# Layer 1 of a four-layer graph attention kernel: the products among the first eleven tiles are formed in the last group of layer 0's gathers, and layer 1 is cut into five blocks

## The chip, the cores and the metric

The kernel runs on one core of one Trainium2 chip. The metric is the device time of one execution in microseconds (us). Times of several runs are given as a median with the lowest and the highest.

## The reference

Four graph attention layers over 3327 nodes with 256 features, one shared adjacency matrix, each followed by a residual addition and a layer norm:

```python
# x: (3327, 256) fp32; adj: (3327, 3327) int32, symmetric, about 1% ones and the diagonal
x = _layernorm(x + _L0_gnn_ref(x, adj, ...))   # GATv2: a . leaky_relu(src_i + tgt_j), softmax over j
x = _layernorm(x + _L1_gnn_ref(x, adj, W, a))  # GAT, one head
x = _layernorm(x + _L2_gnn_ref(x, adj, ...))   # GAT, one head, no leaky_relu
x = _layernorm(x + _L3_gnn_ref(...))           # two GAT layers of four heads of 64

def _L1_gnn_ref(h, adj, W, a):
    Wh = h @ W.T
    s1, s2 = Wh @ a[:256], Wh @ a[256:]
    e = leaky_relu(s1[:, None] + s2[None, :], 0.2)
    e = where(adj == 0, -1e9, e)
    return softmax(e, axis=1) @ Wh
```

In layer 1 row i of the result is a weighted mean of the projected rows j that are neighbours of i. The kernel uses exp(leaky_relu(s1 + s2)), which up to a factor of i is exp(s2) times the larger of a number of i (the "rate") and a number of j. So one vector instruction, max with a scalar of j and then times the adjacency, gives a tile of weights, and a product with the rows of j gives sums over j.

## The kernel before

The nodes are cut into 26 tiles of 128 rows. The program has two parts.

**Layer 0** (`sparse0`) uses that a node has few neighbours. The tiles are handled in four groups, `SETS = (4, 7, 9, 6)`. For a group, `neighbours(s)` finds each row's neighbours by scanning the adjacency, and orders the rows by number of neighbours. Then for each tile POOL gathers, neighbour by neighbour, one row of a table in memory for each of the 128 rows (`gather`, line 912: one indirect transfer of 128 rows of 260 numbers). Gathers are put into parts of up to four; there are 237 parts, of which the last group has 55. One loop goes over the parts. At step q it issues the gathers of part q + 8 (`LEAD`), computes the scores of part q on VectorE (lines 932 and 938), and does what is due at that step. After a tile's last part come the softmax weights (line 976) and `combine`: ScalarE scales gathered rows (line 1014) and TensorE adds them up by products with the identity (line 1017). `put_back` writes a tile's result to memory by an indirect transfer of POOL (line 1051), and `take` reads a group's rows of h back. What is due at a step is listed by `at_step(q, what)`, and within the stage all five engines keep the order in which the program emits instructions.

A tile with the longest lists has an excess: neighbours beyond the seats of a row are spread over other rows (`excess`, `gather_excess`, `score_excess`). `gather_excess` issues two indirect transfers (line 836): the neighbours' rows, and the "own" rows of 773 numbers. Own rows, of the tiles too (`gather_own`, line 897), have four buffers.

While the last group is gathered, the rows of the first 20 tiles (the first three groups, `EARLY`) are already projected for layer 1: `turn_next` transposes a tile on TensorE, `project_next` multiplies it with the weights and sends the features to memory (`feats_d`, line 1154) and the rates of a finished block (`rate1_d`). The first 11 tiles are taken from step `begins[3]` on, one per two steps, and the nine of the third group from `begins[3] + 38` on.

**Layers 1 to 3** (`layers`) are dense. Layers 1 and 2 (`one_head`) go over four blocks of 7, 7, 6 and 6 target tiles. For each source tile j the adjacency of the block comes to the chip (in layer 1 as int32, `ask`, line 135, and ScalarE makes a bf16 copy, line 1651, which it stores to `at_d` for the later layers); VectorE forms the weights (line 1624), and TensorE adds one product of 128x128 by 128x257 to each target tile's sum (line 1718). The adjacency tiles and the weight tiles share eight buffers (tag `e`), the bf16 copies have three. Layer 1's first block reads the features of the first 20 tiles from `feats_d`, three tiles ahead; those of the last six tiles are made within that block, by a list of pieces of work (`pending`) of which one or two are done per source tile (`work_off`). Each later block in the same way carries the norm and the projection for layer 2 of the block before. At the end of a block come the evictions (lines 1739 and 1740). Then, after the first block, the layer 2 object is made: its weights are loaded and VectorE forms two columns of them (`dots`, lines 164 and 165). Layer 3 (`many_heads`) has four heads, twice.

The order of TensorE is that of the program throughout. The other engines keep the program's order until the end of layer 1's first block (`in_order.close()`, `sp_order.close()`); after it a scheduler orders them.

The lines that carry layer 1's loop:

```python
for j in range(nt):
    at = adjacent(j, b, layer is l1)
    e = layer.weigh(j, b, at, 0)
    for s, it in enumerate(block):
        nc.tensor.matmul(accs[s][:pn, : dim + 1], e[:pj, s * P : s * P + pn], f[:pj, : dim + 1], ...)
```

## Time and profile before

| | |
|---|---|
| time, median of 3 runs | 2938.57 us (2932.43 to 2940.5) |
| the profiled execution's own time | 3369.56 us |
| its span, first to last instruction | 3367.8 us |
| TensorE matmul (PE) busy | 2374.6 us, 71% |
| VectorE (DVE) busy | 2134.7 us, 63% |
| ScalarE (ACT) busy | 855.2 us, 25% |
| GpSimd (POOL) busy | 993.0 us, 29% |
| first and last row gather start | 83.6 and 1727.7 us |
| layer 1's products | 1782.9 to 2121.4 us |

The shares are means over stages that have different limits. In a row of the order in time the numbers are start and duration in us, then engine, line and operation, and in brackets how long the engine was idle before it and what ended the wait; "issue" is a wait for which the profile shows nothing, "remote" one whose releaser it cannot name. PEld is TensorE's weight load, which overlaps its matmuls. PEclk is the granted TensorE clock as a share of the full one. An fp32 product is two MATMUL instructions. The profiled execution and the runs that are timed are different executions.

### The profile page before, as it was taken

The page shows a single profiled execution, that of the slowest core. Times are in us where ns is not written, and L with a number is a line of the kernel's source. Part 1 is how long each engine was busy: PE and PEld are TensorE (multiplying, and loading weights), DVE is VectorE, ACT ScalarE, POOL GpSimd, SP SyncE. Part 2 cuts the span into 40 slices and gives each one's busy share as a digit, 9 for nine tenths or more (in the row PEclk, how much of TensorE's full clock was granted, in tenths as well). Part 3 has the DMA queues.
Part 4 walks back from the last instruction along what each step waited for, and adds up shares of the span by engine and source line. Part 5 has one row for each costly group of instructions (what it writes and reads, how often), then busy time and mean ns, then how long its engine had stood idle before and what let it go on. Part 6 is the DMA issues. An engine that isn't in the chain of part 4 may idle for free.

```text
span 3367.8 us, 47149 instructions
## 1 busy us (share of the span) xinstructions
PE 2374.6 (71%) x16703; PEld 1584.2 (47%) x16732; DVE 2134.7 (63%) x5589; ACT 855.2 (25%) x2381; POOL 993.0 (29%) x1061
## 2 busy tenths in 40 slices
PE   7156365453345433444458999999999999999997
PEld 4024243342233332333347788888545656744442
DVE  6278457565466664443554555210689999989997
ACT  3034233232224231322344344111011011111211
POOL 2734644655545666645730000000000000000000
PEclk8557667676666766666779999999999999999998
DMA  7464444433434333324326767333222222222211
GB/s 226 135 178 142 131 121 123 138 103 90 111 101 126 106 91 99 95 78 138 102 62 189 245 197 201 91 107 103 82 64 62 77 75 77 61 67 58 57 48 47
DMA packets 183863, 370.64 MB, mean 110 GB/s; under 512 B 35772, under 2 KB 124707, under 8 KB 182596
## 3 DMA queue, kind: packets, MB, share of 16 engines
q1 hardware_dynamic: 103994, 178.49, 18.9%
q0 software_dynamic: 51008, 155.70, 16.6%
q10 hardware_dynamic: 28618, 33.33, 2.9%
q8 instruction: 137, 2.24, 0.3%
q14 instruction: 106, 0.87, 0.1%
HBM read 327.52 MB, written 46.23 MB: 111 GB/s over the span
## 4 chain that ended last, share of the span: by engine, by line
PE 47%; DVE 16%; issue 13%; another core or an unknown queue 11%; POOL 6%; DMA 4%; ACT 3%; ACTq 0%; DVEq 0%; SPq 0%; POOLq 0%
PE acc L1768 16%; PE acc L1718 13%; PE acc L1776 8%; PE acc L1017 5%; POOL g L912 5%; DVE y L938 4%; DVE y L932 3%; PE misc L1552 2%; DVE e L1624 2%; DVE cand L579 2%; ACT g L1014 1%; DVE found L587 1%; DVE cand L589 1%; DMA at_d<-at 1%
## 5 line engine op out<-in xcount | busy, mean ns | idle before, releaser
L912 POOL DMA_INDIRECT g<-table_d,lst x894 | 851.6, 953 | 417.8 <-issue 259.3
L1624 DVE SCALAR_TENSOR_TENSOR e<-rate,feat,at 128x896 f32<-128x896 f32 (+4 forms) x832 | 843.4, 1078 | 59.7 <-PE acc L1776 47.8
L1768 PE MATMUL acc<-e,feat 128*32 128x384 f32 (+2 forms) x6656 | 692.1, 514 | 2.5 <-DVE e L1624 1.1
L1017 PE MATMUL acc<-g,ident 128*128 128x256 f32 x1766 | 542.0, 468 | 211.6 <-ACT g L1014 86.1
L1017 PEld LDWEIGHTS acc<-g,ident 128*128 128x128 f32 x1766 | 418.2, 242 | 321.3 <-issue 101.3
L938 DVE SCALAR_TENSOR_TENSOR y<-y,a_ps 128x257 f32<-128x257 f32 x894 | 324.6, 418 | 280.6 <-remote 228.0
L1768 PEld LDWEIGHTS acc<-e,feat 128*32 128x32 f32 x6656 | 306.4, 110 | 295.7 <-issue 157.5
L1776 PE MATMUL acc<-e,feat 128*32 128x384 f32 (+3 forms) x3328 | 383.9, 512 | 0.0
L1014 ACT ACTIVATE g<-g,w 128x256 f32<-128x256 f32 x883 | 366.9, 495 | 13.4 <-issue 8.0
L553 PE MATMUL v<-code,leads 65*128 65x512 bf16 (+1 forms) x182 | 88.7, 487 | 326.4 <-remote 134.3
L1718 PE MATMUL acc<-feat,e 128*128 128x257 f32 (+2 forms) x1352 | 303.7, 382 | 8.8 <-DVE inv L1739 5.6
L932 DVE TENSOR_TENSOR y<-g,minus_ps 128x1028 f32<-128x1028 f32 (+2 forms) x233 | 273.0, 1172 | 24.8 <-issue 20.3
L1718 PEld LDWEIGHTS acc<-feat,e 128*128 128x128 f32 (+2 forms) x1352 | 255.1, 191 | 46.3 <-issue 8.0
L1718 PE MATMUL acc<-feat,at 128*128 128x257 bf16 (+2 forms) x2028 | 239.2, 275 | 9.0 <-DMA at<-at_d 8.8
L579 DVE MAX8 cand<-v 128x8 f32<-128x104 f32 (+2 forms) x858 | 168.2, 261 | 98.4 <-issue 90.8
L1776 PEld LDWEIGHTS acc<-e,feat 128*32 128x32 f32 (+1 forms) x3328 | 161.9, 110 | 131.4 <-issue 88.9
L1718 PEld LDWEIGHTS <-at 128*128 128x128 bf16 (+2 forms) x2028 | 199.4, 100 | 43.3 <-DMA at<-at_d 9.5
L1624 DVE SCALAR_TENSOR_TENSOR e<-rate,feat,at_i 128x896 f32<-128x896 f32 (+2 forms) x104 | 112.1, 1079 | 93.8 <-DMA at_i<-in_adj_t_dram 50.8
L1017 PE MATMUL acc<-own_of,ident 128*128 128x256 f32 x52 | 28.6, 651 | 197.9 <-ACT own_of L1014 63.1
L553 PEld LDWEIGHTS <-leads 65*128 65x128 bf16 x182 | 22.8, 125 | 264.2 <-remote 134.2
L1604 POOL DMA_DIRECT2D rate3b_d<-rate_rows x4 | 2.1, 520 | 450.9 <-ACT rate_rows L1603 450.9
L251 POOL TENSOR_TENSOR rstds<-rstds,minus_half 128x7 f32<-128x7 f32 (+1 forms) x8 | 12.1, 1507 | 385.4 <-DVE rstds L250 385.4
(252 smaller groups left out, 1909.1 us busy)
## 6 DMA issues: line engine op xcount, KB each, us to landing
adj_i<-in_adj_dram SPq DMA_DIRECT2D x75, 512.0 KB
at<-at_d SPq DMA_DIRECT2D x150, 224.0 KB
at_i<-in_adj_t_dram SPq DMA_DIRECT2D x50, 448.0 KB
at<-at_d SPq DMA_DIRECT2D x75, 192.0 KB
at<-at_d SPq DMA_DIRECT2D x75, 191.8 KB
g<-table_d,lst POOLq DMA_INDIRECT x894
at_d<-at ACTq DMA_DIRECT2D x50, 224.0 KB
at_i<-in_adj_t_dram SPq DMA_DIRECT2D x25, 384.0 KB
```

The lines of the kernel that those rows point to most:

```text
L553: nc.tensor.matmul(v[:, :w], leads[:, b, :], code[:, :w], start=True, stop=False)
L579: nc.vector.max(spread[:, c0 + c, :], view(v[:, :w]))
L912: nc.gpsimd.indirect_dma_start(out=g[:, k - k0, :], out_offset=None, in_=table_d[:, :], in_offset=bass.IndirectOffsetOnAxis(ap=entry["lst" ...
L932: nc.vector.tensor_tensor(y, rows, minus_src[:, None, :].to_broadcast([P, m, dim + 1]), op=ALU.max)
L938: nc.vector.scalar_tensor_tensor(y, y, 1.0, a_ps[:, : dim + 1], op0=ALU.mult, op1=ALU.mult, accum_out=sc)
L1014: nc.scalar.activation(rows, rows, AF.Copy, scale=w[:, k : k + 1])
L1017: nc.tensor.matmul(dst, ident, rows, start=start, stop=stop)
L1552: nc.tensor.matmul(pacc[:pn, : dim + self.extra], ht[:, k, :pn], self.weight[:, k, :], start=(k == 0), stop=(k == kc - 1),)
L1624: nc.vector.scalar_tensor_tensor(e[:pn, : c1 - c0], self.rate[b][:pn, h_of, : c1 - c0], q, at[:pn, : c1 - c0], op0=ALU.max, op1=ALU.mult,)
L1718: nc.tensor.matmul(accs[s][:pn, : dim + 1], a[:pj, s * P : s * P + pn], f[:pj, : dim + 1], start=(j == 0 and part == 0), stop=(j == nt - 1 ...
L1768: nc.tensor.matmul(accs[x][p][q : q + 32, : hi - lo], f[:pj, at0 : at0 + 32], es[at0 // hd][:pj, lo:hi], start=(j == 0), stop=(j == nt - 1),)
L1776: nc.tensor.matmul(accs[x][pairs][h_of * 32 : (h_of + 1) * 32, : hi - lo], f[:pj, dim + h_of : dim + h_of + 1].to_broadcast([pj, 32]), es[ ...
```

## The change

Layer 1 is cut into five blocks instead of four, along the groups: tiles 0-4, 5-10, 11-14, 15-19 and 20-25 (`blocks1`). They are handled in the order 11-14, 0-4, 5-10, 15-19, 20-25 (`order1`).

The products whose source and target tiles are both among the first eleven (`KNOWN` = 11) are formed in the last group of layer 0. The targets are taken in sets of up to three (0-2, 3-4, 5-7, 8-10), for each set the eleven source tiles one per step, 44 steps from `begins[3] + 2` on. `ask_early` loads adjacency and features two steps ahead on SP's queue, `weigh_early` makes the bf16 copy on ScalarE, stores it to `at_d` and forms the weights on VectorE, `add_early` makes up to three products one step later, and `keep_early` copies finished sums out and stores them to `part_d`. In layer 1 the blocks 0-4 and 5-10 then start at source tile 11; their parts are loaded at the block's start and added by products with the identity at source tile 15.

The first eleven tiles are projected 25 steps earlier, with the loads that this takes.

The own rows of the excess are no longer gathered: `send_own` makes them by a product with a permutation from the tile's own rows.

The layer 2 object is made at source tile 9 of layer 1's first block and the layer 3a object at source tile 15; their `dots` become single steps (`fold`) at one per source tile from four tiles later. At the end of a layer 1 block the first two edge tiles of the next block are formed ahead of the evictions (`ready`), and the sums of successive blocks take PSUM banks in rotation. Rates of layer 1's five blocks share four buffers: block 20-25 uses that of block 11-14.

The core of the diff:

```diff
+    KNOWN = sum(SETS[:-2])
+    blocks1 = []
+    for lo, hi in ((0, KNOWN), (KNOWN, EARLY), (EARLY, nt)):
+        count = -(-(hi - lo) // 6)
+        ends = [lo + (hi - lo) * c // count for c in range(count + 1)]
+        blocks1 += [list(range(a, b)) for a, b in zip(ends, ends[1:])]
+    order1 = sorted(range(len(blocks1)), key=lambda b: (blocks1[b][0] != KNOWN, b))
...
-                for dst, src, x in ((own, own_d[s], 1), (g[:, 0, :], table_d, 0)):
-                    nc.gpsimd.indirect_dma_start(
-                        out=dst, out_offset=None, in_=src[:, :],
-                        in_offset=bass.IndirectOffsetOnAxis(ap=over["rows"][:, x : x + 1], axis=0),
-                    )
+                nc.gpsimd.indirect_dma_start(
+                    out=g[:, 0, :], out_offset=None, in_=table_d[:, :],
+                    in_offset=bass.IndirectOffsetOnAxis(ap=over["rows"][:, :1], axis=0),
+                )
+
+            def send_own(s):
+                over = extras[s]
+                over["own"] = early_bank()
+                nc.tensor.matmul(
+                    over["own"][:, : dim + 1], over["forth"], held[s, 0]["own"][:, : dim + 1],
+                    start=True, stop=True,
+                )
...
+            def ask_early(m):
...
+                t = find.tile([P, PIECE], I32, tag="adj_i", name="at_f", bufs=3)
+                f = t[:, BANK : BANK + dim + 2].bitcast(F32)
+                copy_rows(nc.sync, t[:, :w], adj_t[j * P : (j + 1) * P, lo : lo + w])
+                nc.sync.dma_start(f, feats_d[j * P : (j + 1) * P, :])
+                asked1[m] = t, f
+
+            def weigh_early(m):
...
+                at = find.tile([P, 3 * P], BF16, tag="cand", name="at1")
+                nc.scalar.copy(at[:, :w], t[:, :w])
+                nc.scalar.dma_start(at_d[j * P : (j + 1) * P, lo : lo + w], at[:, :w])
+                x = m % 3 * 3 * P
+                e = formed1[m] = state1["e"][:, x : x + w]
+                nc.vector.scalar_tensor_tensor(
+                    e, state1["rate"][:, :w], f[:, dim + 1 : dim + 2], t[:, :w],
+                    op0=ALU.max, op1=ALU.mult,
+                )
+
+            def add_early(m):
...
+                if j == 0:
+                    state1["accs"] = [early_bank() for _ in trio]
+                for s, acc in enumerate(state1["accs"]):
+                    nc.tensor.matmul(
+                        acc[:, : dim + 1], e[:, s * P : (s + 1) * P], f[:, : dim + 1],
+                        start=(j == 0), stop=(j == KNOWN - 1),
+                    )
+
+            def keep_early(m):
+                for s, it in enumerate(pairs1[m][0]):
+                    y = find.tile([P, dim + 1], F32, tag="minus", name="part1")
+                    nc.scalar.copy(y, state1["accs"][s][:, : dim + 1])
+                    nc.scalar.dma_start(part_d[it * P : (it + 1) * P, :], y)
...
-            at = begins[len(SETS) - 1]
+            at = begins[len(SETS) - 1] - 2 * KNOWN - 3
...
+            at = begins[len(SETS) - 1] + 2
+            at_step(at - 2, ask_early, 0)
+            at_step(at - 1, ask_early, 1)
+            for m, (trio, j) in enumerate(pairs1):
+                at_step(at, add_early, m - 1)
+                if j == 0 and m:
+                    at_step(at + 1, keep_early, m - 1)
+                    at += 1
+                at_step(at, weigh_early, m)
+                at_step(at, ask_early, m + 2)
+                at += 1
...
-                rate = (rates if b else head_p).tile(
-                    [P, heads, len(blocks[b]) * P], F32, tag=f"r{b}", name="rate"
+                blocks = self.blocks
+                x = self.order.index(b) % 4
+                rate = (rates if x else head_p).tile(
+                    [P, self.nh, len(blocks[b]) * P], F32, tag=f"r{x}", name="rate"
                 )
...
-            for b, block in enumerate(blocks):
+            for turn_b, b in enumerate(layer.order):
+                block, first = layer.blocks[b], turn_b == 0
+                skip = first_of(layer, b)
                 work_until(lambda: not layer.leaky or layer.rate[b] is not None)
-                accs = [bank(s) for s in range(len(block))]
-                for j in range(nt):
+                accs = [bank((used + s) % 7) for s in range(len(block))]
+                used += len(block)
+                parts = ask_parts(block) if skip else ()
+                for j in range(skip, nt):
...
+                    if skip and j == skip + LATER:
+                        for acc, y in zip(accs, parts):
+                            nc.tensor.matmul(
+                                acc[:, : dim + 1], ident, y, start=False, stop=False
+                            )
...
-                    elif j >= LATER:
+                    elif j >= skip + LATER:
                         work_off()
+                    if first and j in make:
+                        made.append(make[j]())
+                        folds += [(j + 4 + i, step) for i, step in enumerate(made[-1].fold())]
+                    while folds and folds[0][0] <= j:
+                        folds.pop(0)[1]()
                 work_until(lambda: not pending)
-                in_order.close()
+                if layer is l1 and turn_b + 1 < len(layer.order):
+                    then = layer.order[turn_b + 1]
+                    work_until(lambda: layer.rate[then] is not None)
+                    at0 = first_of(layer, then)
+                    for j in range(at0, at0 + 2):
+                        ready[j] = fetched(j, then)
...
-        one_head(l1, second, (7,))
-        l2 = made[0]
-        l3a = Layer("l3a", "f", heads, True, load_heads(l3_w1, l3_a1), rate_d=rate3_d[0])
-        one_head(l2, lambda: l3a, (7,))
+        one_head(l1, {9: second, 15: third}, (7,))
+        l2, l3a = made
+        one_head(l2, {}, (7,))
```

## The prediction

> **What bounds the kernel now.** I read the page first (span, the rows by slice), then the busy time by stretch, then POOL's rows, then the chain of waits and the order of instructions around layer 1.
>
> ```profile
> span 3367.8 us, 47149 instructions
> PE   7156365453345433444458999999999999999997
> POOL 2734644655545666645730000000000000000000
> PEclk8557667676666766666779999999999999999998
> ```
>
> Two kernels in one: for 21 slices no engine is full and TensorE is granted 0.6 to 0.7 of its clock; from there PE is full to the end. The busy time by stretch (us, and instructions in brackets, for PE, PEld, DVE, ACT, POOL; then clock, DMA share, GB/s) puts the border at 1782 us:
>
> ```profile
> 1374.00:1728.00 354.00, 148.19 (x513) 115.94 (x512) 166.67 (x593) 95.04 (x278) 211.17 (x222) 0.67 0.39 104
> 1728.00:1782.00 54.00, 43.69 (x194) 34.04 (x192) 32.43 (x109) 36.09 (x115) 2.66 (x3) 0.99 0.11 31
> 1782.00:1877.00 95.00, 87.61 (x402) 74.21 (x402) 37.65 (x61) 31.98 (x59) 4.63 (x6) 1.00 0.77 241
> 1877.00:1960.00 83.00, 77.37 (x355) 66.83 (x356) 49.69 (x96) 33.76 (x58) 1.50 (x1) 0.96 0.72 215
> ```
>
> The first row is the last group's gathers, the second their tail, the third layer 1's first block. In the gather stage POOL issues one indirect transfer after another; two rows of its order in time, and the statistics of the line:
>
> ```profile
> 1510.59 0.95 POOL L912 DMA_INDIRECT g<-table_d,lst  x1 [0.30 <-issue]
> 1511.84 0.94 POOL L912 DMA_INDIRECT g<-table_d,lst  x1 [0.30 <-issue]
> ...
> L912 POOL DMA_INDIRECT g<-table_d,lst x894: 941/949/1562, 83.6 to 1727.7; - x179
> ```
>
> One costs 0.95 + 0.30 = 1.25 us. There are 894 + 8 + 26 + 26 + 22 = 976, so POOL's floor is 1220 us; the profiled stage (83.6 to 1728) took 1644. The profiled execution took 3369.56 us (span 3367.8 and 1.8 around it), 431 more than the median of 2938.57. Layers 1 to 3 (1782.9 to 3367.8, 1585 us) run with PE full, so I place the 431 us ahead of them: without profile 2938.6 - 1.8 - 1585 - 83.6 - 54 (tail) leaves 1214 us for the gathers, POOL's floor within 6 us. The stage without profile is then POOL's alone, and the long stalls that the waits put down to nobody belong to the profile:
>
> ```profile
> DVE y L938 <- remote: 228.0, 43, 27.2
> POOL g L912 <- PE acc L1017: 64.9, 21, 18.8
> ```
>
> This inference carries the forecast; a rival below drops it.
>
> **Layer 1 before.** The order of PE in time:
>
> ```profile
> 1849.09 27.57 PE L1718 MATMUL acc<-feat,e 128*128 128x257 f32 x126
> 1882.26 2.05 PE L1718 MATMUL acc<-feat,e 128*128 128x257 f32 x4 [5.59 <-DVE inv L1739]
> ...
> 2026.24 2.77 PE L1718 MATMUL acc<-feat,e 128*128 128x257 f32 x12
> 2028.84 1.03 PE L1552 MATMUL misc<-l2w,turned 128*128 128x257 f32 x4
> ```
>
> A product is two instructions; six take 2028.84 - 2026.24 = 2.60 us, 0.434 each. Layer 1 runs from 1782.9 to 2121.4, 338.5 us, with 26 x 26 = 676 products (293.4). The first block ends at 1876.7: 182 products are 79.0 of its 93.8, so 14.8 for projecting the last six tiles; 5.6 idle; then 494 products are 214.4 of 239.1, so 24.7 for layer 2's projections.
>
> **The change, part by part.**
> *Products moved.* 11 x 11 = 121 leave layer 1: -52.5. Eleven additions of a 128x257 part, same shape as a product: +4.8.
> *The block boundary.* Layer 2's and 3a's weight columns (dots) are now formed inside the first block, so the 5.6 us go: DVE then had waited for l_att and done both layers' dots ahead of the evictions. The next block's first two edge tiles are now formed before the evictions; the other boundaries cost 0.4 to 0.6 each and I leave them. Sum so far: -53.3.
> *The first block gets shorter than what feeds it.* It has 4 target tiles, 4 x 0.434 = 1.74 us of PE per source tile instead of 3.04. The chain of waits there:
>
> ```profile
> 1788.26 6.78 DMA h<-sums_d
> ...
> 1798.27 5.21 DMA at_d<-at
> 1803.51 0.95 ACT at L1651
> 1804.48 5.03 DMA at_d<-at
> ```
>
> ACT's casts stand behind the loads of h until 1795.9 and then go three buffers per store: (5.0 + 0.95) / 3, 2.0 us per source tile. PE was at source tile 5 at 1799.5; with 4 tiles it would be there at 1782.9 + 8.7 = 1791.6. So +7 waiting there, and about +2 over the next six at a store of half the size: +9 (0 if h comes 9 us sooner than in the profile, since then nothing is late; 16 if the loads that DVE waits on slow down as much again beside 0.5 MB per 1.74 us, 295 GB/s against the 241 of the row).
> *Rates.* Block 20-25's rates now take the first block's buffer (r0), and their load stands on POOL's queue ahead of those of blocks 0-4, 5-10 and 15-19. It waits for DVE's last weighing of the first block. DVE led PE by three source tiles before (last weighing 1867.5, PE done 1876.7), so 5.2 us at 1.74 each; two issues, a landing like the 4.6 us of at_i on the chain, and a weighing are 9: +4 (0 to 9).
> *Layer 2's projections* in the second and third block have 11 steps of work for 12 and 14: a last turn and projection stand alone, +2. Parts loaded from memory hold two of eight edge buffers for four source tiles; three source tiles in flight at 2.17 us still cover a 4.6 us load: 0.
> Layer 1: -53.3 + 9 + 4 + 2 = -38.
> *Excess seats.* Four own-row gathers on POOL (0.95 + 0.30) become a product on PE: -5. Fewer users of the four own buffers can save POOL waits: 0 taken, 10 at most (one wait of 9.8 us for hs is seen in the last group).
> *The early work*, 44 steps in the last group's 55: 121 products, 44 weighings, 44 casts with stores, 88 loads on SP, 11 parts stored on ACT's queue. Without profile the group has 222 x 1.25 = 278 us. PE: 148 + 121 x 0.434/0.67 = 148 + 78 = 226. DVE: 167 + 33 x 0.57 + 11 x 0.42 (between 0.42 for 257 and 1.15 for 896 columns) = 190. ACT: 95 + 44 x (0.45 + 0.36 issue) + 11 x 0.75 = 139. DMA: 19 MB more over 278 us, 69 GB/s beside 122, share about 0.7, below the 0.77 that layer 1 runs at; gathers have eight pieces' lead, 40 us, over a landing under 4 us on the chain. All fit, so 0. The projections of the first eleven tiles and layer 1's weight loads go 25 steps earlier, beside the building of the last group's lists: 11 tiles at 1.1/0.67 us of PE and 1.4 of ACT in 22 steps of 5 us, the same work in the same stage, 0 (a few us if PE's product makes DVE's scans late). SP's queue holds nothing else urgent then: the feature stores of tiles 11 to 19 and layer 1's first loads stand behind the early loads, which wait for PE's product one step back. The cover is thinnest in the last third, where three of four spare PSUM banks hold sums and turns and projections share the fourth, PE waiting for ACT (about 1.2 us per pair, as in the tail now) with products beside it: two steps are 3.7 + 1.1 + 1.2 + 2.6 = 8.6 us at full clock against 10 of POOL, 12.3 at 0.67. Between 0 and 14 late at the tail; I take +3, since a fuller PE is granted more clock in the page (0.99 in the tail).
>
> **A rule that speaks against it.** DVE's two-input row L1042 (0.42 us from 1509.04) ran into a POOL issue at 1509.27 that took 1.01 us, against 0.95. The Trainium skill, "SBUF — State Buffer", section Who interferes with whom, says that a DVE instruction with two SBUF inputs contends with a GpSimd instruction that reads SBUF, the later one blocking wholly. The early weighing has two SBUF inputs, and gathers read their index list from SBUF: 23 us of weighings would hold POOL up to 23 us. By the row it is 44 x 0.06, under 3. I take the row as 0 and keep 23 for the range.
>
> **Sum.** -38 - 5 + 3 = -40 against the profiled execution's own 3369.6 where its stage were POOL's; the same difference on the median gives 2938.6 - 40 = 2898.6, say 2899. A profile of the changed kernel may hide part of it in its own stalls.
>
> **Rivals.**
> *Feeding bound (0.15).* The first block is wholly paced by loads and stores: about 16.6 MB at 241 GB/s is 69 us, and with a late rate load and port blocking half real, gain 15 to 25: about 2918. For: DMA already 0.77 busy. Against: loads alone ran faster than the mean.
> *Slower (0.10).* The gather stage is a chain through DVE, ACT and PE and not POOL's: POOL was busy 211 of 354 us, and waited for PE's buffers 65 us. Then the early products come on top, in full 78 us, against 38 + 5 gained elsewhere: +35, 2974. It decides once more than 43 of the 78 are uncovered. Against: the 1214 us above.
> *More (0.10).* First block and rates in time, own buffers free: -53 + 2 - 5 - 10 = -66, 2873.
> *It does not do what it says:* the five blocks still make 555 + 121 products; only their place changes, and PE's order shows the 121 among the last gathers. I give this none.
> The likeliest (0.65) spans 2885 to 2912. A run of this kernel spreads 8 us, so 0.3% (9 us) is what can be told from none. Faster 0.84, same 0.07, slower 0.09. The range 2870 to 2926 leaves out the slower case and the far end of the gain.
>
> **What would show it.** Right: layer 1 near 300 us; PE idle 5 to 13 us in its first block with releasers h, at_d or at_i; a wait of a few us for rate at the second block; 0.43 us per product; POOL at 0.30 between issues beside the early weighings. Wrong: POOL issues over 1 us beside them, many POOL waits for "PE acc" in the last group, a tail longer than 54 us by over 14, or a layer 1 above 315 us.

## The result, and the profile after

The changed kernel takes 2907.94 us (median of 4 runs, 2905.49 to 2911.82) against 2937.18 for the kernel before beside it: ratio 0.9903, 95% interval 0.9884 to 0.9921, or 29 us less. A second set of runs gave 2910.12, ratio 0.9903 (0.9886 to 0.9920). The forecast was 2899, range 2870 to 2926.

The profiled execution took 2906.56 us (span 2904.8), so this page, unlike that of the kernel before, is that of the runs timed. Its span and the same three rows:

```profile
span 2904.8 us, 47707 instructions
PE   6466657555552665767899999999999999999997
POOL 2676777777777777772000000000000000000000
PEclk9577778777776887889999999999999999999998
```

POOL stands at 6 to 7 tenths through nearly the whole gather stage, where the page of before showed 4 to 6: 0.95 of every 1.25 us is busy, so 7 tenths is POOL issuing with hardly a pause. The chain of waits of the page gives "another core or an unknown queue" 0%, against 11% before.

The busy time by stretch (columns as before) for the last group's gathers, their tail and the first block of layer 1:

```profile
1020.00:1296.00 276.00, 177.74 (x682) 141.31 (x681) 171.47 (x573) 112.83 (x296) 210.28 (x219) 0.80 0.67 184
1296.00:1350.00 54.00, 39.36 (x169) 30.61 (x167) 34.18 (x114) 30.05 (x93) 22.92 (x24) 0.94 0.53 135
1350.00:1420.00 70.00, 57.95 (x246) 46.41 (x246) 29.38 (x65) 23.73 (x59) 5.15 (x7) 0.95 0.74 219
```

The early work is in the first row: the clock granted is 0.80 and the transfers, gathers among them, move 184 GB/s (122 without the early work, in five_blocks). POOL's statistics, and its order in time beside one early weighing:

```profile
L926 POOL DMA_INDIRECT g<-table_d,lst x894: 942/949/1309, 80.8 to 1322.4; - x179
...
1206.99 0.94 POOL L926 DMA_INDIRECT g<-table_d,lst  x1 [0.30 <-issue]
1208.24 0.98 POOL L926 DMA_INDIRECT g<-table_d,lst  x1 [0.30 <-issue]
1209.53 0.94 POOL L926 DMA_INDIRECT g<-table_d,lst  x1 [0.30 <-issue]
...
1208.32 0.61 DVE L1221 SCALAR_TENSOR_TENSOR e<-rate,at_f 128x384 f32<-128x384 f32 x1
```

From first to last gather are 1241.6 us. The floor is 972 issues (four own-row gathers fewer than before) at 1.25, 1215; POOL's waits for PE's sums add 18.0 and for landings 8.8: 1242. The stage is POOL's, in this execution.

Layer 1, in PE's order, at its start and at the second and third block:

```profile
1350.57 5.44 PE L1845 MATMUL acc<-feat,e 128*128 128x257 f32 x24 [1.13 <-issue]
1359.15 8.89 PE L1845 MATMUL acc<-feat,e 128*128 128x257 f32 x32 [3.14 <-DVE e L1728]
...
1422.21 6.32 PE L1845 MATMUL acc<-feat,e 128*128 128x257 f32 x20 [3.02 <-DVE e L1728]
...
1474.36 9.76 PE L1845 MATMUL acc<-feat,e 128*128 128x257 f32 x36 [3.98 <-DVE e L1728]
...
1659.80 1.17 PE L1845 MATMUL acc<-feat,at 128*128 128x257 bf16 x9
```

The last row is layer 2. Layer 1 runs from 1350.57 to 1659.8, 309.2 us, against 338.5 before: 29.3 us, as much as the whole measured gain (two smaller parts ahead of it nearly cancel, below). The block at 1474 starts its third source tile 3.98 us late, a wait that the prediction has no term for.

### The profile page after: what moved, and what is told of

The parts are those of the page before. It is cut to its first block, busy times and chain, and to the rows that moved or that the text cites. A ratio compares the mean times of both kernels' runs of the same rounds, so it can differ in the third digit from the quotient of the medians.

```text
span 2904.8 us, 47707 instructions
## 1 busy us (share of the span) xinstructions
PE 2310.4 (80%) x16735; PEld 1545.7 (53%) x16764; DVE 2128.0 (73%) x5634; ACT 866.0 (30%) x2441; POOL 991.7 (34%) x1059
## 4 chain that ended last, share of the span: by engine, by line
PE 53%; DVE 8%; POOL 6%; DMA 6%; issue 5%; ACT 2%; ACTq 0%; SPq 0%; DVEq 0%; POOLq 0%; another core or an unknown queue 0%
PE acc L1913 18%; PE acc L1845 14%; PE acc L1921 9%; PE acc L1031 7%; POOL g L926 5%; DVE e L1728 3%; DMA g<-table_d,lst 3%; PE misc L1653 3%; DMA at_d<-at 1%; DVE y L952 1%; ACT g L1028 1%; DMA at<-at_d 1%; DVE y L946 1%; PE early L1234 1%; PE misc L1765 0%
## 5 line engine op out<-in xcount | busy, mean ns | idle before, releaser
L926 POOL DMA_INDIRECT g<-table_d,lst x894 | 853.9, 955 | 275.8 <-issue 237.6
L1031 PE MATMUL acc<-g,ident 128*128 128x256 f32 x1766 | 484.5, 430 | 70.7 <-ACT g L1028 47.1
L1031 PEld LDWEIGHTS acc<-g,ident 128*128 128x128 f32 x1766 | 378.9, 219 | 158.2 <-ACT g L1028 64.9
L1028 ACT ACTIVATE g<-g,w 128x256 f32<-128x256 f32 x883 | 367.5, 495 | 15.1 <-ACT at L1217 10.6
L1845 PE MATMUL acc<-feat,e 128*128 128x257 f32 (+1 forms) x1110 | 257.5, 388 | 15.8 <-DVE e L1728 14.6
L1845 PEld LDWEIGHTS acc<-feat,e 128*128 128x128 f32 (+1 forms) x1110 | 211.6, 194 | 50.9 <-DVE e L1728 15.3
L1845 PEld LDWEIGHTS <-at 128*128 128x128 bf16 (+2 forms) x2028 | 199.6, 100 | 42.4 <-issue 4.7
L563 PE MATMUL v<-code,leads 65*128 65x512 bf16 (+1 forms) x182 | 79.7, 438 | 144.2 <-DVE cand L589 103.3
L589 DVE MAX8 cand<-v 128x8 f32<-128x104 f32 (+2 forms) x858 | 157.1, 258 | 1.1 <-PE v L566 1.1
L1728 DVE SCALAR_TENSOR_TENSOR e<-rate,feat,at_i 128x640 f32<-128x640 f32 (+4 forms) x108 | 95.9, 899 | 82.3 <-DMA at_i<-in_adj_t_dram 27.7
L261 POOL TENSOR_TENSOR rstds<-rstds,minus_half 128x6 f32<-128x6 f32 (+3 forms) x9 | 12.4, 1381 | 357.8 <-DVE rstds L260 357.8
```

The source lines that it names most:

```text
L563: nc.tensor.matmul(v[:, :w], leads[:, b, :], code[:, :w], start=True, stop=False)
L589: nc.vector.max(spread[:, c0 + c, :], view(v[:, :w]))
L926: nc.gpsimd.indirect_dma_start(out=g[:, k - k0, :], out_offset=None, in_=table_d[:, :], in_offset=bass.IndirectOffsetOnAxis(ap=entry["lst" ...
L1028: nc.scalar.activation(rows, rows, AF.Copy, scale=w[:, k : k + 1])
L1031: nc.tensor.matmul(dst, ident, rows, start=start, stop=stop)
L1728: nc.vector.scalar_tensor_tensor(e[:pn, : c1 - c0], self.rate[b][:pn, h_of, : c1 - c0], q, at[:pn, : c1 - c0], op0=ALU.max, op1=ALU.mult,)
```

## The experiments

In the table, "to layer 1" runs from the first gather to layer 1's first product; the gathers themselves start between 77 and 86 us from one execution to the next, so the difference is the steadier figure. "Gathers" is from the first to the last one, "tail" from there to layer 1. Each of these columns comes from one execution. The rest of the kernel, layers 2 and 3, takes 1241 to 1250 us in the profiles of all runs, so the medians are the safer measure of a whole kernel and the columns of a part.

| kernel | us | ratio to before (95%) | gathers | tail | to layer 1 | layer 1 |
|---|---|---|---|---|---|---|
| changed | 2907.94 | 0.9903 (0.9884-0.9921) | 1241.6 | 28.2 | 1269.8 | 309.2 |
| changed_again | 2910.12 | 0.9903 (0.9886-0.9920) | 1240.3 | 25.8 | 1266.1 | 309.6 |
| five_blocks | 2946.08 | 1.0025 (1.0016-1.0035) | 1239.6 | 22.7 | 1262.3 | 352.5 |
| early_twice | 2915.45 | 0.9927 (0.9906-0.9947) | 1244.6 | 34.9 | 1279.5 | 307.0 |
| rates_apart | 2907.37 | 0.9895 (0.9876-0.9914) | 1243.0 | 25.4 | 1268.4 | 310.6 |
| three_ready | 2901.56 | 0.9868 (0.9848-0.9888) | 1240.9 | 25.1 | 1266.0 | 303.7 |
| own_again | 2935.17 | 0.9984 (0.9976-0.9991) | 1239.6 | 22.1 | 1261.7 | 339.4 |
| third_part_again | 2904.67 | 0.9888 (0.9873-0.9903) | 1241.4 | 23.3 | 1264.7 | 309.2 |
| three_edits | 2894.35 | 0.9852 (0.9834-0.9870) | 1240.9 | 24.5 | 1265.4 | 304.3 |

Four runs (own_by_product, third_part_apart, take_on_pool, all_four) were made together on a chip where the kernel before took 3344.4 us: the long stalls with no known releaser, which the profile of before had shown too, are there in the timed runs as well. Of these four only layer 1, which has no such stalls, is read beside the others.

**Five blocks without the early work.**

```
-            pairs1 = [(trio, j) for trio in trios for j in range(KNOWN)]
+            pairs1 = []
...
-            return KNOWN if early and layer is l1 and layer.blocks[b][-1] < KNOWN else 0
+            return 0
```

> The changed kernel with its five blocks and their order, but with no early products: all 676 products are formed in layer 1, and no part is stored or loaded. Theory A (the gather stage is POOL's alone, so the early work costs nothing there and all of the gain is layer 1's): 121 products come back at 0.434 us, 52.5, less eleven additions, 4.8, and less the 2 us of projections left over in the short blocks, so 2908 + 46 = 2954 us, 17 above the kernel before; the first gathers and the last lie where they lie in the changed kernel (80.8 and 1322 us), within 4 us. Rival B (the early work costs about 9 us in the gather stage and its tail, which is why 29 us were gained where 40 were forecast): 2945 us, and the last gather is issued about 9 us earlier.

Measured: 2946.1, near rival B's 2945. Its layer 1 is 352.5 us: the early products are worth 352.5 - 309.2 = 43.3 us there. Its layer 1 begins 1262.3 us after the first gather, where the four kernels with unchanged early work (changed twice, rates_apart, three_ready) need 1266.0 to 1269.8, mean 1267.6. So the early work costs 5 to 6 us ahead of layer 1: 1.9 in the gathers (mean 1241.5 against 1239.6), 3.7 in the tail (mean 26.1 against 22.4, own_again with it); the four differ by 3.8 us among themselves, so this is good to some 2 us. Theory A's "costs nothing" is wrong by that much. Rival B has the total but not the place: the last gather is issued 1.2 us earlier (1321.2 against 1322.4), where it said 9. Theory A was right in that part, and missed the total because layer 1 gave 43 where it had 46 and the tail was not free. Five blocks alone are worse than four: layer 1 is 14 us longer than before, the products being the same 676. The earlier projections, which this kernel keeps, cost nothing that shows: own_again, without them, needs 1261.7 us to layer 1.

**Every early product twice.**

```
+                    for again in range(2):
                         nc.tensor.matmul(
...
-                            start=(j == 0), stop=(j == KNOWN - 1),
+                            start=(j == 0 and not again), stop=(j == KNOWN - 1 and again == 1),
...
-                    nc.scalar.copy(y, state1["accs"][s][:, : dim + 1])
+                    nc.scalar.mul(y, state1["accs"][s][:, : dim + 1], 0.5)
```

> The changed kernel with each of the 121 early products formed twice into the same sum, which is halved where it is stored. Theory A (POOL paces the gathers): 121 more products are 53 us of PE at full clock, 66 at the 0.80 granted in the last group, and lie beside POOL's gathers: within 5 us of 2908, layer 1 unchanged. Rival B (the early work is on the path of the gather stage): 20 to 66 us longer, 2928 to 2974, with POOL waiting for PE in the last group.

Measured: 2915.5, by the medians 5 to 8 us more, though the intervals of the ratios overlap. The last group and its tail show what became of 121 more products:

```profile
1020.00:1296.00 276.00, 209.02 (x879) 173.46 (x877) 170.15 (x570) 111.85 (x294) 210.16 (x218) 0.88 0.67 182
...
1332.95 6.59 PE L1031 MATMUL acc<-g,ident 128*128 128x256 f32 x16 [4.10 <-ACT g L1028]
```

PE is busy 209 us of 276 and POOL is as busy as before (210.16): the gathers take 1244.6 us, 3 more. What does not fit comes out in the tail, 34.9 us, because the last sums of the group begin late (1332.95, where the changed kernel has them at 1324.13). From the first gather to layer 1 it is 11.9 us more than the mean above. So most of the early work is covered, as theory A has it, and the cover ends in the last third of the group, as the prediction said; that is rival B in a small size. POOL's waits for PE's sums do not grow (17.4 us against 18.0), which rival B had named.

**A separate place for the late rates.**

```
+                if self is l1 and self.order.index(b) >= 3:
+                    if not shared:
+                        shared.append(rates.tile([P, 2, wide], F32, tag="r3", name="rate"))
+                    at0 = self.order.index(b) - 3
+                    rate = shared[0][:, at0 : at0 + 1, : len(blocks[b]) * P]
```

> The changed kernel with the rates of block 20-25 in a buffer of their own (half of the one that block 15-19 uses), so that their load no longer waits for the last weighing of the first block, and the loads behind it on POOL's queue don't either. Theory A (the late rates cost the second block 3 to 5 us: DVE waits 7.58 us for rate at 1421 us, PE 3.0 at 1422): the wait for rate goes, layer 1 is 3 to 5 us shorter, 2904 us. Rival: the evictions of the first block and the three norms ahead of them hold the weighings just as long, and nothing is gained, 2908.

Measured: 2907.4, no gain; the rival's outcome holds, but by edge loads first, which it did not name. DVE at the end of the first block, in the changed kernel and then in this one:

```profile
1421.27 1.68 DVE L1728 SCALAR_TENSOR_TENSOR e<-rate,feat,at_i 128x640 f32<-128x640 f32 x2 [7.58 <-DMA rate<-rate_d]
```

```profile
1415.85 0.75 DVE L1734 SCALAR_TENSOR_TENSOR e<-rate,feat,at_i 127x512 f32<-127x512 f32 x1 [5.84 <-DMA at_i<-in_adj_t_dram]
1417.05 0.88 DVE L1734 SCALAR_TENSOR_TENSOR e<-rate,feat,at_i 128x640 f32<-128x640 f32 x1 [0.45 <-DMA at_i<-in_adj_t_dram]
...
1424.94 0.41 DVE L267 TENSOR_SCALAR h<-h,mvs,rstds 128x256 f32<-128x256 f32 x1 [1.15 <-POOL rstds L261]
1426.07 0.88 DVE L1734 SCALAR_TENSOR_TENSOR e<-rate,feat,at_i 128x640 f32<-128x640 f32 x1 [0.72 <-DMA at_i<-in_adj_t_dram]
```

The rates are in time, but now the edge loads are not, and then the norm stands between the weighings: PE's waits around the second block are 1.21, 0.56, 0.17 and 2.82 in place of 3.02 and 0.86.

**Three source tiles ready.**

```
-                    for j in range(at0, at0 + 2):
+                    for j in range(at0, at0 + 3):
```

> The changed kernel with the edge tiles of three source tiles, not two, formed ahead of the evictions at each block boundary of layer 1. Theory A (at the third block PE waits 3.98 us at 1474 us because the evictions of the block before, five or six of two instructions each, stand on DVE between the second and the third source tile's weighing): that wait shrinks to below 1.5 us, the 1.29 at the fifth block goes too, and the whole is 4 to 6 us shorter, 2903 us. Rival: the third weighing ahead only delays the evictions and the norms behind them, or waits for edge buffers (eight, of which three source tiles take six), and PE waits one source tile later: 2908.

Measured: 2901.6, some 6 to 9 us less; the intervals of the ratios just touch. DVE in the changed kernel, ahead of the late product at 1474:

```profile
1466.45 1.01 DVE L1728 SCALAR_TENSOR_TENSOR e<-rate,feat,at_i 128x768 f32<-128x768 f32 x1
1467.38 0.48 DVE L1883 SCALAR_TENSOR_TENSOR h<-acc,inv,h 128x256 f32<-128x256 f32 x1
...
1470.23 0.17 DVE L260 TENSOR_SCALAR rstds<-mvs 128x5 f32<-128x5 f32 x1
1471.68 1.70 DVE L267 TENSOR_SCALAR h<-h,mvs,rstds 128x256 f32<-128x256 f32 x5 [1.28 <-POOL rstds L261]
1473.30 2.87 DVE L1728 SCALAR_TENSOR_TENSOR e<-rate,feat,at_i 128x768 f32<-128x768 f32 x3
```

After the second weighing of the new block come not only the evictions, as my theory had it, but the whole norm of the block before: its statistics, 1.28 us waiting for POOL, which takes the power for the norm's scale, and five normalisations of 1.70 in all. PE's row there with a third tile ahead, and the busy time of the third block (from the end of the last product of the block before to that of its own) in the changed kernel and in this one:

```profile
1468.97 3.30 PE L1845 MATMUL acc<-feat,e 128*128 128x257 f32 x14 [1.88 <-DVE e L1728]
```

```profile
1463.26:1515.99 52.73, 48.23 (x218) 41.22 (x216) 27.99 (x61) 19.54 (x37) 1.16 (x1) 0.97 0.64 189
```

```profile
1456.87:1506.32 49.45, 46.81 (x218) 39.97 (x216) 28.04 (x61) 19.44 (x37) 1.16 (x1) 1.00 0.67 196
```

PE waits 1.88 (and 0.24 one source tile earlier) instead of 3.98 us, and the block takes 49.5 us instead of 52.7. The waits make 1.9 us of these 3.3; the other 1.4 is the clock. In the changed kernel the granted clock stands at half for 3.4 us after the long wait, so that the same 218 instructions keep PE busy 48.23 us instead of 46.81:

```profile
1474.60:1478.00 3.40, 3.40 (x9) 2.70 (x9) 1.57 (x2) 0.22 (x1) 0.00 (x0) 0.51 0.87 268
```

Two parts of the expectation failed: the wait is not below 1.5, and the 1.29 at the fifth block stays (1.29 again). Layer 1 as a whole is 5.5 us shorter, 2.8 of it PE's busy time (283.1 against 285.9 us for the same products; two such stretches at half clock instead of four) and 2.7 its waits (20.6 against 23.3). Not all of that is the edit's doing: the first block is 3.8 us shorter, and that of kernels with the same first block lies anywhere from 64.8 to 68.6, for a reason found in part only (see the last loads of h, below).

**The own rows alone, in the kernel before.**

```
-                for dst, src, x in ((own, own_d[s], 1), (g[:, 0, :], table_d, 0)):
...
+                nc.tensor.matmul(
+                    over["own"][:, : dim + 1], over["forth"], held[s, 0]["own"][:, : dim + 1],
+                    start=True, stop=True,
+                )
```

> The kernel before with one part of the change alone: the own rows of the excess seats come by a product on PE from the row tile at hand, not by four gathers on POOL. Theory A (POOL paces the gather stage): the stage is 4 x 1.25 = 5 us shorter, and up to 10 more if the freed own buffers end waits; layer 1 unchanged at 338 us; 2937.7 - 5 = 2932.7 us, layer 1 starting at about 1345. Rival (the stage without profile is a chain of other engines, and the four gathers lie in its gaps): 2937.7, layer 1 starting at 1350.

3311.6 against 3344.4 on the chip with stalls (ratio 0.9911, 0.9895 to 0.9926): neither of the expected figures applies. On a chip without the stalls:

> The kernel before with the own rows of the excess seats by product alone, a second time, since its first run fell on a chip where all kernels take 400 us longer and said nothing of POOL's floor. Where the kernel before takes near 2938: theory A gives 4 x 1.25 = 5 us and a few us of ended waits, 2931 us, with layer 1 starting at about 1344 (the run of five blocks without early work started it at 1343.9). Rival (POOL's gain is nothing and the six us came from the earlier projections of five_blocks): 2938, layer 1 starting at 1350. Where the gathers stall: near 3312 again.

2935.2 against 2939.2, ratio 0.9984: by the ratio 4.7 us less, between 2.6 and 7.1. Theory A's 5 us. Layer 1 is 339.4 us, so all of it lies ahead of it. (It began at 1347.9, not 1344, with its first gather at 86.2.)

**The third part in another ring.**

```
-                    y = find.tile([P, dim + 1], F32, tag="minus", name="part1")
+                    if s < 2:
+                        y = find.tile([P, dim + 1], F32, tag="minus", name="part1")
+                    else:
+                        y = io0.tile([P, ROW], F32, tag="row", name="part1", bufs=3)[:, : dim + 1]
```

It is aimed at these rows of ACT in the changed kernel, where the third part waits for a buffer and eight scalings for the third part:

```profile
1322.79 0.37 ACT L1242 COPY part<-early 128x257 f32<-128x257 f32 x1 [3.45 <-DMA part_d<-part]
1323.20 0.33 ACTq L1243 DMA_DIRECT2D part_d<-part  x1
1323.57 3.30 ACT L1028 ACTIVATE g<-g,w 128x256 f32<-128x256 f32 x8 [0.40 <-ACT part L1242]
```

> The changed kernel with the third of three parts copied into a buffer of another ring, not the first part's. Theory A (the early work's cost of 6.7 us in the tail is the last store: ACT waits 3.45 us at 1319.8 us for the first part's store to land before it can copy the third, and the last gathers' scalings stand behind it on ACT's queue): ACT's wait goes, layer 1 starts 3 to 5 us sooner, at 1346 to 1347 us, 2904 us. Rival (the tail is late because PE is behind with the early products themselves): layer 1 starts within 1 us of 1350.6, 2908.

> The changed kernel once more, beside the third part's edit on one chip. Where the kernel before takes near 2938: 2908 us, layer 1 starting 1268 us after the first gather (mean of its three runs so far, counting the two kernels that have the same gather stage). Where the kernel before takes near 3344: if the stalls fall on the early work as on everything else, the same 29 us less, 3315; if the stage there is a chain through other engines, the own rows give 33 us and layer 1 gives 32, and the early work takes some 35 back, again near 3315, but with layer 1 starting as late as in the kernel before.

> The changed kernel with the third of three parts in another ring, a second time, since the first run fell on a chip with stalls and told nothing of the tail. Where the kernel before takes near 2938: theory A (ACT's wait for the first part's store holds the last scalings): layer 1 starts 2 to 4 us sooner after the first gather than in the changed kernel beside it, 2904 to 2906 us. Rival (PE's own backlog of early products makes the tail): no difference beyond 1 us, 2908. Where the gathers stall: no difference that can be told.

The first run (3317.9, ratio 0.9921) fell on the chip with stalls. On one without them:

```profile
1316.10 0.38 ACT L1245 COPY part<-early 128x257 f32<-128x257 f32 x1 [0.40 <-DMA feats_d<-feat]
1316.50 0.33 ACTq L1246 DMA_DIRECT2D part_d<-part  x1
1316.88 3.31 ACT L1028 ACTIVATE g<-g,w 128x256 f32<-128x256 f32 x8 [0.40 <-ACT part L1245]
```

The wait is gone, and the way to layer 1 is 1264.7 us against 1266.1 beside it, the tail 23.3 against 25.8: 1.4 to 2.5 us, the low end of theory A. One execution of each does not prove it, since the tails of the four kernels without the edit lie between 25.1 and 28.2 and that of three_edits, which has it, at 24.5. The medians are 5.4 us apart, but their intervals overlap. By these figures about half of the tail's 3.7 us is this wait; the rest may be PE's own backlog, which lengthens the tail in early_twice.

**The last loads of h on POOL's queue.**

```
-                    copy_rows(nc.scalar, h[it][:pn], sums_d[s][t * P : t * P + pn, :])
+                    copy_rows(nc.gpsimd if s == len(SETS) - 1 else nc.scalar, h[it][:pn], sums_d[s][t * P : t * P + pn, :])
```

> The changed kernel with the last group's loads of h issued on POOL's queue, not ACT's. Theory A (in the first block ACT's casts of at stand behind 6.65 us of h loads at 1355.7, and the edge buffers behind the casts): the casts run on, PE's waits in the first block fall from 10.6 to about 5 us, 2903 us. Rival (the block is paced by its loads, which wait for memory that the last scatter frees at 1354.5 us): PE's waits stay within 2 us, 2908.

On the chip with stalls, 3316.5 (0.9918). Its first block:

```profile
1765.28 0.32 SPq L2187 DMA_DIRECT2D feat<-feats_d  x1
1765.45 3.87 POOL L146 DMA_DIRECT2D h<-sums_d  x7 [2.00 <-DMA sums_d<-hs,lst]
1765.45 0.62 ACT L1755 CAST at<-at_i 128x512 bf16<-128x512 int32 x1 [6.23 <-DMA sums_d<-hs,lst]
1765.65 0.42 SPq L146 DMA_DIRECT2D at_i<-in_adj_t_dram  x1
1766.49 0.62 ACT L1755 CAST at<-at_i 128x512 bf16<-128x512 int32 x1 [0.42 <-ACT at L1755]
```

The casts do run on at once, and PE's waits stay: 9.5 us in this block of 65.9 us, against 10.3 and 65.7 in third_part_apart on the same chip, with the loads on ACT's queue (10.6 and 68.6 in the changed kernel). The rival holds: features, edge tiles, casts and loads of h all start together when the last group's last scatter has landed, and ACT waits 6.23 us for that scatter (6.22 in the changed kernel). So the first block's start hangs on the scatter; that this is because memory is reused, as the rival has it, is not shown. And ACT's order is not cleared altogether. In the nine profiles with the seven h loads on ACT's queue, the loads take ACT 4.8 to 5.3 us in six, and the first block 64.8 to 66.7; they take 6.3 to 7.1 us in three, the changed kernel twice and rates_apart, and the block 68.4 to 68.6. third_part_apart is one of the six (5.09 us). Whether the slow loads hold the casts there, or both are slowed by something else, these runs don't tell.

**All four, and the three that act.**

> The changed kernel with all four edits: rates of block 20-25 apart, three source tiles ready at each boundary, the third part in another ring, the last h loads on POOL. If they act apart: 3 at the second block (with the weighings ahead of the evictions the rates' wait is no longer covered by them), 3 to 5 at the third, 3 to 5 at the tail, 4 in the first block: 2908 - 14 = 2894 us. If the casts and loads just wait on each other in another place: 2901, as with three source tiles ready alone.

> The changed kernel with three edits: the third part in another ring, three source tiles ready at each boundary, the rates of block 20-25 apart. Expected beside the kernel before on the same chip. Where the gathers run without long stalls (kernel before near 2938): layer 1 near 302 us (309.2 - 1.7 - 3.1 at its second and third block, as in the run of all four) and its start 3 to 5 us sooner than the changed kernel's 1350.6: 2908 - 5 - 4 = 2899 us, ratio 0.987. Rival (PE's own backlog makes the tail): 2903, layer 1 starting at 1350. Where the gathers stall (kernel before near 3344): 3312, as all four gave.

All four gave 3312.3 on the chip with stalls (0.9913), layer 1 302.4 us, with 42.4 and 49.4 for its second and third block. The three gave 2894.35, ratio 0.9852: 45 us less than the kernel before and 14 to 16 less than the changed kernel, and faster than both, somewhat more than expected. That it beats three_ready alone is not shown: the intervals overlap, its layer 1 is no shorter (304.3 against 303.7, where 302 was expected) and begins 1265.4 us after the first gather against 1266.0. Its second block takes 41.3 us (44.1 in the changed kernel and with three tiles ready, 43.9 with the rates apart); 1.3 us of that is waits, the rest a clock of 1.00 instead of 0.96. Since all_four shows a short second block too, the two edits seem to need each other here: the rates in time are of use only once three weighings stand ahead of the norm. In three_edits part of the gain is lost again in its third block, at a clock of 0.97.

## Why the prediction was right, and where 11 us of its gain were missing

**The inference on the gather stage: right in its use, wrong in its cause.** Without stalls the stage is POOL's: own_again's gathers take 1239.6 us for 972 issues, 1215 at 1.25, and the page's row for POOL there is

```profile
L919 POOL DMA_INDIRECT g<-table_d,lst x894: 942/950/1612, 86.2 to 1325.8; - x179
```

But the stalls do not belong to the profile. In one set, on one chip, all 34 executions of five kernels stalled (the kernel before 3344 us), and on the three other chips on record none of 123 stalled (the longest took 2977 us). Whether the chip or the moment decides, and what causes the stalls, stays open. The figure that carried the inference was in part luck. 1214 us lies below POOL's own floor of 1220, which cannot be: the tail of 54 us was that of a stalled execution and is 22 undisturbed, and the gathers take 1240. The two errors, 32 and 26 us, nearly cancel.

**Layer 1, -38 forecast, -29.3 measured.** This is the mis-sized term. By blocks, worked out with the prediction's own figures (0.434 a product, 1.23 = 24.7/20 for projecting a tile for layer 2) against the profile. A block runs from the end of the last product of the block before to that of its own; the waits are PE's, the clock is the granted one:

| block | its terms | forecast | measured | waits | clock |
|---|---|---|---|---|---|
| 11-14 | 104 products, 14.8, feeding 9 | 68.9 | 68.6 | 10.6 | 0.95 |
| 0-4 | 75 and 5 parts, 4 tiles, rates 4 | 43.6 | 44.1 | 3.9 | 0.96 |
| 5-10 | 90 and 6 parts, 5 tiles | 47.9 | 52.7 | 4.5 | 0.97 |
| 15-19 | 130, 6 tiles, left over 2 | 65.8 | 67.8 | 2.0 | 1.00 |
| 20-25 | 156, 5 tiles | 73.9 | 76.0 | 2.3 | 1.00 |

The products moved (43.3 in five_blocks against 45.7 forecast with the 2 left over), the feeding of the first block and the rates are right within 2.5 us. Two steps failed.

The first is "The next block's first two edge tiles are now formed before the evictions; the other boundaries cost 0.4 to 0.6 each and I leave them". I took the boundaries from the old order and did not ask what comes behind the two tiles: the evictions and the norm now stand between the second weighing and the third. PE waits 3.98 us for that weighing in the third block, and the fifth has 2.3 us of waits for weighings. (The 2.0 in the fourth are waits for ACT in the projections left over from the third, which the forecast had. That block is over its terms because more of the projections fall into it: PE's order has 3, 4 and 8 tiles in the second to fourth block, where the terms have 4, 5 and 6.)

The second is 0.434 for every product, which holds at full clock. The rows of the third block in three_ready's account give the price of one stretch of 3.4 us at half clock: 1.4 us. The changed kernel has four of them in layer 1, the one shown there and these, two in the first block and one in the second:

```profile
1358.60:1362.00 3.40, 2.85 (x7) 2.33 (x8) 1.20 (x2) 0.00 (x0) 0.00 (x0) 0.50 0.92 296
1382.50:1385.90 3.40, 3.40 (x10) 2.66 (x9) 2.92 (x6) 0.81 (x2) 0.00 (x0) 0.50 0.89 268
1423.40:1426.80 3.40, 3.40 (x9) 2.35 (x8) 3.34 (x15) 0.00 (x0) 0.00 (x0) 0.51 0.67 210
```

The profile of the kernel before has one of 6.8 us, beside its wait of 5.6 us. By estimate, 1.4 us for each 3.4, the clock is some 3 us of the 9 that are missing. The first block's 68.6 is then right for other reasons than forecast: of the 9 us of feeding, 4.5 are more waits than before (10.6 against 6.1) and some 2.6 are the clock (PE busy 57.95 us, against 55.39 in three_ready's first block at 1.00).

Two more reasons inside right numbers were off. The +9 of the first block was put down to casts behind h loads; take_on_pool shows no gain from moving those loads, since everything waits for the last scatter first; at most some 3 us, in the executions with slow loads, can be theirs. The +4 for the rates is the wait the trace shows, but taking it away alone gains nothing, since edge loads and the norm are as late.

**Own rows, -5:** -4.7 measured (-2.6 to -7.1), so little or nothing more from freed buffers. **Early work, 0 and tail +3:** +1.9 and +3.7. **Port rule, 0 by the row, up to 23 by the rule:** POOL's 894 gathers take 853.9 us with 44 early weighings and 853.0 in five_blocks without; 0.98 for the issue that a weighing ran into. The row was right, and on this pair of instructions the rule did not show, within 1 to 2 us in all.

The sum, as measured: -29.3 - 4.7 + 5.6 = -28.4, beside the medians' -29. The terms ahead of layer 1 are 3 us worse than forecast, layer 1 is 9 worse.

**The rivals.** Not feeding bound: the first block is as forecast. The slower one, early products coming on top of the gather stage, holds in a tenth: 5.6 us of the 53 that the products take at full clock. With the stalls it may weigh more: there the own rows alone gained 33 us, while the three kernels with the early work, whose layer 1 is 33 to 37 us shorter than own_by_product's, gained 26 to 32 in all; so they lost as much again ahead of layer 1, where the early work is. Their profiles agree: from the first gather to layer 1 they need 1672 to 1682 us, own_by_product 1629 (in the fastest execution of its set), and their tails are 72 to 77 us against 57. So beside stalled gathers most of the early work seems uncovered, as the slower rival had it, and the gain was saved by own rows that are worth more there. No run on that chip takes the early work out alone, so this is not shown. Of the signs named beforehand, PE's idle time in the first block (10.6 us), the wait for rates and POOL at 0.30 beside the weighings came; layer 1 lies between the mark for right, 300, and that for wrong, 315. The tail limit of "54 and 14" was worthless: undisturbed the tail is 22 us, not 54.

## What to carry to other kernels

Work moved beside a stage that one queue paces is nearly free, as long as that queue does pace it, until the last pieces of that stage, where there is nothing left to hide behind. It should end earlier (not tried here), and none of its stores should share a two-buffer ring with the tail's engine. When a change puts something ahead of a known block boundary, read what then stands behind it in that engine's order; a boundary's old price does not hold for a new order. Count a wait of some 3 us on TensorE with the slower clock behind it, here another 1.4 us. A saved wait counts only if the second latest thing is in time, so waits on one spot are tried together as well as one by one.

## What the runs showed of the hardware that was not expected

The same kernel took 2938 us in most sets of runs and 3344 in one. Single engines stood for up to 27 us in the stage of indirect transfers with no releaser on record while POOL went on issuing, as in these 25 us of the profile of before and the DVE row that ends them:

```profile
1428.00:1453.00 25.00, 0.00 (x0) 0.00 (x0) 0.00 (x0) 0.00 (x0) 16.11 (x18) 0.52 0.39 96
...
1453.45 0.42 DVE L938 SCALAR_TENSOR_TENSOR y<-y,a_ps 128x257 f32<-128x257 f32 x1 [27.21 <-remote]
```

Layer 1 ran at the same pace with such a stage ahead of it and without (339.7 us in own_by_product, 339.4 in own_again).

More work on PE raised the clock it was granted: in the 276 us of the last group 0.73 with 123 us busy (five_blocks), 0.80 with 178 (changed), 0.88 with 209 (early_twice). From 1020 us to layer 1 PE is busy 155 us without early products, 217 with them and 261 with each made twice:

```profile
1020.00:1343.86 323.86, 154.99 (x614) 123.56 (x614) 184.20 (x641) 119.69 (x342) 231.66 (x242) 0.75 0.46 118
```

```profile
1020.00:1350.57 330.57, 217.10 (x849) 171.94 (x848) 206.19 (x685) 142.87 (x387) 233.21 (x242) 0.82 0.65 175
```

```profile
1020.00:1360.44 340.44, 261.36 (x1105) 216.12 (x1104) 207.59 (x690) 146.35 (x397) 235.65 (x243) 0.89 0.62 171
```

The second set of 121 products cost 44 us of PE, not 53 or 66, and the first 62. In layer 1 the clock went the other way with PE's waits. Over all fourteen profiles, each of the 24 waits of 2.6 us or more came with at least 3.4 us at half clock, beginning within 3.6 us of the wait's end; of nine waits between 1.8 and 2.3 us four did, and no shorter one of over 1 us. The Trainium skill, "TensorE: Matmul & The Clock Gate", Part 1, has the clock halved by default and released by activity, which agrees; what a stage of short pieces is granted on the mean only these rows tell.
